# Moving two additions from VectorE to GpSimd in a four-layer graph network, with a new pace, the overflow test ahead of the last normalisations, and layer 2's first loads ahead of the general path

## The chip, the cores and the metric

The kernel runs on one core of one Trainium2 chip. The metric is the device time in microseconds; the kernel before took 4518.02 us (median of 3 runs, 4509.77 to 4524.34). TensorE is written PE, VectorE DVE, ScalarE ACT, GpSimd POOL and SyncE SP, as in the profile.

## The reference

Four graph layers run over N = 2708 nodes with C = 128 features and a sparse adjacency matrix `adj` (2708 x 2708, f32, about five non-zero entries per row). Each layer is `x = x + L(relu(layernorm(x)))`.

```
L0: d = adj.sum(1); (adj * d^-1/2 rows and columns) @ (h @ W + b)
L1: q, k, v = (h @ W.T).reshape(128, N, 8)          # 128 heads of width 8
    a = softmax(q k^T / sqrt(128) + 2 adj);  out = (a v) @ Wo.T
L2: agg = adj.T @ h / deg;  y = agg @ Wn.T + bn + h @ Wc.T + bc
    relu(batchnorm(y) over the nodes)
L3: for each pair (i, j): s = sum_f sigmoid(a_j + b_i + b1) * adj_ij;  sum_j s * h_j;  @ weight + bias
```

The rest of this text is about layer 1 and the start of layer 2.

## The kernel before, in words

Rows of nodes are cut into NT = 22 tiles of 128 (the last has 20). Layer 1 does not form the N x N attention of a head. Its logits are small, so exp(q.k) is replaced by a polynomial: each key is expanded into 128 features (`fk`), each query likewise (`fq`), a head's keys and values become one moment matrix, and the queries are evaluated against it. What the adjacency adds, exp(2 adj) - 1 at the few neighbours of a node, is summed apart, from gathered rows. A test at the end of the layer asks whether the logits and the neighbour counts stayed within the polynomial's limits; if not, three hardware loops (`tc.For_i` with a count of 0 or more, read from `flag`) do the layer again in general form. With these inputs the counts are zero.

**The head loop** (L1106 to L1163) is written out by hand under `tc.manual_schedule()`, so each engine gets its instructions in program order. It has D = 128 heads of NCH = 6 rounds ("chunks", at most four row tiles each). GpSimd makes the key features of head d+2 in round 0 (`keys`, L1015, `mul_g`, L1010) and the products `y` of keys and values in rounds 2 and 5 (`with_values`, L1021). TensorE accumulates the moments of head d+1 (`moments`, L1048), transposes query features (`turn`, L1074) and evaluates head d (`evaluate`, L1086). VectorE weights the moments (`mw`, L1058), makes query features (`fq`, L1007) and, per round, multiplies what was evaluated by the query terms (`z`, L1094) and sums it (`o_raw`, L1100). ScalarE copies transposed features out of PSUM (`fT`, L1076). For every four heads GpSimd adds the sum of the values (`sums`, L693) and SP stores the group (`o_g`).

**Side work** is a chain of Python generators, `first` (L956 to L959). Per round `PACE` steps of it are taken, one step being the code up to the next `yield` (L1150 to L1154). It has four parts in this order:

- `search` and `by_node`, by turns: ten row tiles of adjacency are searched for their largest entries on VectorE (`neighbours`, L128), and q, k and v are stored again by node, 32 groups of heads.
- `in_order` sorts the nodes by their number of neighbours.
- `from_neighbours` (L802) handles 121 slots; slot e of a row tile is the e-th neighbour of its nodes. A slot is: `load` of the next slot (indirect gather on GpSimd's queue, L825, three buffers), `logits` (product `c_z`, L840, and sum `c_c`, L844, both VectorE), and `values` of the slot before (a copy on ScalarE into the ninth column, L869; the product `c_v`, L870; and, except for the first slot of a tile, the addition `c_acc + c_v`, L878, on VectorE). `weigh` (L852, L854) is ScalarE's. A finished tile's `c_acc`, which has one buffer, is scattered to `more_n` (L887, GpSimd's queue). `c_z` and `c_v` share one tag with two buffers.

When `first` is used up, each round takes up to three calls of `step` (L975) on `beside`, a list of two kinds of work: `normalise(g)` (L917) for a group of four heads and `project_out` (L496) for a row tile. `normalise` loads the group and the neighbours' part (L921, L922), adds them (L930, VectorE), takes the reciprocal (L932), multiplies (L933) and stores with twelve or thirteen transfers (L399). `project_out` loads a tile (L499), multiplies with Wo (L505) and adds to `x_sb` (L508). A group may only be normalised once the loop is two groups beyond it, at most two pieces of work are under way, and each has to wait `WAIT = 3` rounds after its loads. What is left when the heads are done is taken after the loop (L1164).

**After the loop** come the test (L1183 to L1225: small reductions on VectorE with five transposes or products on TensorE), the reading of `flag` by all engines, the three loops of the general path (L1229, L1241 to L1295, L1295), and layer 2: loads of two weight matrices and four vectors, `norm_relu` (L192), the reciprocal degrees `di`, 22 steps that spread them over a matrix (`dg` on VectorE, `d_ps` on TensorE, `diB` on ScalarE, L1329 to L1332), and the aggregation `adj.T @ h`: 22 row tiles of adjacency (1354 KB each, four buffers, L1339) against `h` (L1341).

Outside `manual_schedule` blocks the scheduler of the framework chooses each engine's order, within the dependences.

Of the kernel before, what the change touches and what calls it, by code (L numbers as in the profile page):

```python
# [9 lines left out]
FP = mybir.dt.float32  # L10
# [6 lines left out]
P = 128  # L17
# [32 lines left out]
def gnn4_kernel(  # L50
# [75 lines left out]
    few = keep.tile([P, 1], FP, name="few")  # L126

# [388 lines left out]
    with ExitStack() as ph:  # L516
# [285 lines left out]
        def from_neighbours():  # L802
# [55 lines left out]
            def values(b):  # L858
# [6 lines left out]
                for e in range(w):  # L865
# [10 lines left out]
                    yield  # L876
                    if s0 + e:
                        nc.vector.tensor_tensor(acc[:sz], acc[:sz], z[:sz], ALU.add)  # L878
                        yield
# [37 lines left out]
        def normalise(g):  # L917
# [12 lines left out]
            nc.vector.tensor_tensor(ro, ro, co, ALU.add)  # L930
# [67 lines left out]
        PACE = 1.30  # L998
# [107 lines left out]
        with tc.manual_schedule():  # L1106
# [19 lines left out]
            for d in range(D):  # L1126
# [35 lines left out]
                if (d + 2) % GRP == 0 and (d + 2) // GRP + 1 < NG:  # L1162
                    soon.append(prepare((d + 2) // GRP + 1, got))  # L1163
            while beside or under_way:  # L1164
                if not step(n, NG):
                    n += 1


    with ExitStack() as ph:
        gp = ph.enter_context(tc.tile_pool(name="l1g", bufs=1))  # L1170
        gw = ph.enter_context(tc.tile_pool(name="l1g_w", bufs=2))
        g_l = ph.enter_context(tc.tile_pool(name="l1g_l", bufs=1, space=PSUM))
        g_t = ph.enter_context(tc.tile_pool(name="l1g_t", bufs=1, space=PSUM))
        g_o = ph.enter_context(tc.tile_pool(name="l1g_o", bufs=1, space=PSUM))
        q_f = dram.tile([N, P, HEAD], FP, name="q_f")
        k_f = dram.tile([N, P, HEAD], FP, name="k_f")
        v_f = dram.tile([N, P, VW], FP, name="v_f")
        o_f = dram.tile([N, P, HEAD], FP, name="o_f")

        nc.vector.memset(top, 0.0)  # L1183
        p2 = gp.tile([C, 2], FP, name="p2")
        for e in range(2):
            pt = g_t.tile([P, BK], FP, name="g_tr", tag="tr")
            nc.tensor.transpose(pt[:C, :P], most2[:, e], ident)
            nc.vector.tensor_reduce(p2[:, e : e + 1], pt[:C, :P], axis=AX.X, op=ALU.max)
        nc.vector.tensor_tensor(top[:, 0:1], p2[:, 0:1], p2[:, 1:2], ALU.mult)
        nc.vector.tensor_tensor(top[:, 1:2], p2[:, 0:1], p2[:, 1:2], ALU.max)  # L1190
        nc.vector.tensor_reduce(top[:, 2:3], nval, axis=AX.XY, op=ALU.max)
        nc.vector.tensor_reduce(top[:, 3:4], nval, axis=AX.XY, op=ALU.min)
        low = gp.tile([P, 1], FP, name="low")
        nc.vector.tensor_reduce(low, least, axis=AX.X, op=ALU.min)
        nc.vector.tensor_tensor(top[:, 3:4], top[:, 3:4], low, ALU.min)
        nc.vector.tensor_scalar_mul(top[:, 3:4], top[:, 3:4], -1.0)
        nc.vector.tensor_reduce(low, below, axis=AX.X, op=ALU.max)
        nc.vector.tensor_tensor(top[:, 3:4], top[:, 3:4], low, ALU.max)
        nc.vector.tensor_tensor(top[:, 3:4], top[:, 3:4], full, ALU.max)
        pt = g_t.tile([P, BK], FP, name="g_tr", tag="tr")  # L1200
        nc.tensor.transpose(pt[:4, :P], top, ident)
        t4 = gp.tile([4, 1], FP, name="top4")
        nc.vector.tensor_reduce(t4, pt[:4, :P], axis=AX.X, op=ALU.max)
        pt = g_t.tile([P, BK], FP, name="g_tr", tag="tr")
        nc.tensor.transpose(pt[:1, :4], t4, ident[:4, :4])
        bnd = gp.tile([1, 6], FP, name="bound")
        nc.vector.tensor_copy(bnd[:, :4], pt[:1, :4])
        nc.vector.tensor_scalar(
            bnd[:, 4:5], bnd[:, 0:1], MAX_LOGIT**2, None, ALU.is_le
        )  # L1210
# [391 lines left out]
```

## Time and profile before

| what | value |
|---|---|
| median of 3 runs | 4518.02 us (4509.77 to 4524.34) |
| the profiled execution | 4486.52 us, span 4484.7 us |
| mean granted TensorE clock | 0.837 |
| busy, share of the span: PE / DVE / ACT / POOL | 72% / 82% / 25% / 57% |
| first and last start of `mw` (heads 0 and 127) | 465.7 and 3907.1 us |
| first `c_z`, last `c_acc` | 1383.0 and 3524.0 us |
| first and last addition of a normalisation (L930) | 3543.5 and 3999.9 us |
| last addition to `x_sb` of layer 1 (L508) | 4018.1 us |

The spans come from one profiled execution, which was 0.7% faster than the median of the three timed runs; sums made from the profile are sums against 4486.52. The busy share is an average over stages with different limits, so the stages are looked at one by one. In a row of a group, "busy" is the sum over all instructions of the group, "mean ns" one of them, and what follows the bar is how long the engine was idle just before these instructions and what ended that. [...] Line numbers are those of the kernel before; in the kernel after, the lines up to the head loop stand one further down.

### The profile page before, as it was taken

How to read it: one execution, taken by the hardware profiler on the slowest of the kernel's cores; microseconds unless marked ns; L12 is line 12 of the kernel's file. 1: busy time of each engine (PE TensorE's matmuls, PEld its weight loads, DVE VectorE, ACT ScalarE, POOL GpSimd, SP SyncE). 2: the span in 40 equal slices, each digit the busy share in tenths (PEclk: the TensorE clock that was granted, in tenths of full speed). 3: DMA queues.
4: the chain of work that ended last, by engine and by line, in shares of the span. 5: the costliest groups of instructions: out<-in, count | busy, mean ns of one | idle time of the engine just before them, and what ended most of it. 6: DMA issues, size and time to landing. Idle time of an engine off the chain costs nothing. (4 is left out here: it accounts for less than half of the span.)

```text
span 4484.7 us, 49573 instructions
## 1 busy us (share of the span) xinstructions
PE 3225.3 (72%) x17298; PEld 2876.7 (64%) x17298; DVE 3669.4 (82%) x4983; ACT 1100.2 (25%) x2497; POOL 2544.8 (57%) x2253
## 2 busy tenths in 40 slices
PE   7985778889966677677777676667676687839634
PEld 5952777788856666667666676667666677824323
DVE  5988889998868999999999998999899888831323
ACT  4255233334412222222222222222122111101201
POOL 0001766678858666677676676767576555300076
PEclk9987888999988888888888888888888788959555
DMA  4647334357702222222222222222222344447132
GB/s 186 227 154 294 86 101 110 87 126 171 164 9 84 79 75 76 89 81 83 87 76 88 77 92 78 85 86 94 86 88 88 76 97 95 107 108 262 51 100 79
DMA packets 402005, 480.24 MB, mean 107 GB/s; under 512 B 290672, under 2 KB 322098, under 8 KB 376916
## 3 DMA queue, kind: packets, MB, share of 16 engines
q1 hardware_dynamic: 370140, 308.03, 23.8%
q0 software_dynamic: 31600, 168.86, 11.2%
q8 instruction: 144, 2.36, 0.2%
q14 instruction: 121, 0.99, 0.1%
HBM read 363.13 MB, written 113.67 MB: 106 GB/s over the span
## 5 line engine op out<-in xcount | busy, mean ns | idle before, releaser
L1086 PE MATMUL g_ps<-mw,fT 128*128 128x189 f32 x5632 | 1213.3, 362 | 734.6 <-DVE mw L1058 501.9
L1086 PEld LDWEIGHTS g_ps<-mw,fT 128*128 128x128 f32 x5632 | 1032.8, 213 | 812.8 <-issue 642.2
L1010 POOL TENSOR_TENSOR y<-bk,raw 128x2079 f32<-128x2079 f32 x256 | 982.9, 3840 | 685.7 <-PE m_ps L1048 658.4
L1048 PE MATMUL m_ps<-y,fk 128*128 128x189 f32 (+1 forms) x5632 | 1108.1, 342 | 29.0 <-POOL y L1010 29.0
L1048 PEld LDWEIGHTS m_ps<-y,fk 128*128 128x128 f32 (+1 forms) x5632 | 969.2, 204 | 58.1 <-POOL y L1010 29.5
L1076 ACT COPY fT<-f_ps 128x512 f32<-128x512 f32 (+1 forms) x768 | 422.9, 551 | 1955.2 <-PE f_ps L1074 1954.3
L1094 DVE TENSOR_TENSOR z<-g_ps,bq 128x756 f32<-128x756 f32 (+1 forms) x768 | 669.1, 871 | 177.7 <-PE g_ps L1086 173.9
L1100 DVE TENSOR_REDUCE o_raw<-z 128x36 f32<-128x756 f32 (+1 forms) x768 | 672.5, 876 | 26.3
L1010 POOL TENSOR_TENSOR fk<-bk,raw 128x528 f32<-128x528 f32 (+1 forms) x512 | 526.5, 1058 | 0.0
L1074 PE MATMUL f_ps<-ident,fq 128*128 128x128 f32 x2816 | 490.8, 299 | 46.2 <-DVE fq L1007 44.6
L1074 PEld LDWEIGHTS f_ps<-ident,fq 128*128 128x128 f32 x2816 | 399.2, 157 | 83.9 <-issue 45.8
L1010 POOL TENSOR_TENSOR fk<-raw,bk 128x352 f32<-128x352 f32 (+1 forms) x512 | 337.3, 688 | 0.0
L840 DVE TENSOR_TENSOR c_z<-c_kv,c_q 128x1024 f32<-128x1024 f32 (+1 forms) x121 | 308.1, 2546 | 5.3 <-DMA c_kv<-kv_n,srt 5.3
L1007 DVE TENSOR_TENSOR fq<-bq,q_ps 128x528 f32<-128x528 f32 (+1 forms) x512 | 288.1, 605 | 0.0
L825 POOL DMA_INDIRECT c_kv<-kv_n,srt x121 | 139.1, 1150 | 244.3 <-DVE c_v L870 142.4
L1010 POOL TENSOR_TENSOR bk<-raw 128x88 f32<-128x88 f32 (+1 forms) x512 | 238.3, 496 | 34.6 <-DMA raw<-qkv_c 34.1
L878 DVE TENSOR_TENSOR c_acc<-c_acc,c_v 128x1152 f32<-128x1152 f32 (+1 forms) x99 | 248.2, 2507 | 2.5
L465 POOL MEMSET qkv<- 128x512 f32 x6 | 6.3, 1076 | 373.7 <-PE l_o L350 254.3
L870 DVE TENSOR_TENSOR c_v<-c_kv,c_c 128x1024 f32<-128x1024 f32 (+1 forms) x99 | 205.9, 2080 | 0.0
L1420 POOL DMA_INDIRECT g<-gate_d,srt x121 | 122.0, 1008 | 107.9 <-issue 105.1
L505 PE MATMUL l_o<-woT,o_cr 128*128 128x128 f32 (+1 forms) x352 | 94.8, 425 | 107.6 <-DMA o_cr<-o_c 68.6
L1007 DVE TENSOR_TENSOR fq<-q_ps,bq 128x352 f32<-128x352 f32 (+1 forms) x512 | 171.7, 378 | 0.0
(284 smaller groups left out, 3490.2 us busy)
## 6 DMA issues: line engine op xcount, KB each, us to landing
a_nat<-in_adj_dram SPq DMA_DIRECT2D x32, 1354.0 KB
qkv_c<-qkv SPq DMA_DIRECT2D x5, 6400.0 KB
a<-in_adj_dram SPq DMA_DIRECT2D x21, 1354.0 KB
kv_n<-n_kv SPq DMA_DIRECT2D x32, 672.0 KB
an<-in_adj_dram SPq DMA_DIRECT2D x15, 1354.0 KB
o_g<-o_raw SPq DMA_DIRECT2D x32, 396.0 KB
r_raw<-o_g SPq DMA_DIRECT2D x32, 396.0 KB
r_more<-more_n SPq DMA_DIRECT2D x32, 396.0 KB
```

Source lines behind the costliest of these rows:

```text
L825: nc.gpsimd.indirect_dma_start(out=kvs[b][:sz, e].rearrange("p c e k -> p (c e k)"), out_offset=None, in_=kv_n.rearrange("n c k -> n (c k) ...
L840: nc.vector.tensor_tensor(z[:sz], kvs[b][:sz, e, :, 0], qs[t][:sz], ALU.mult)
L870: nc.vector.tensor_tensor(z[:sz, :, :HEAD], kv[:sz, e, :, 1], c[:sz, e, :, None].to_broadcast([sz, C, HEAD]), ALU.mult,)
L878: nc.vector.tensor_tensor(acc[:sz], acc[:sz], z[:sz], ALU.add)
L1007: nc.vector.tensor_tensor(o, x, y, ALU.mult)
L1010: nc.gpsimd.tensor_tensor(o, x, y, ALU.mult)
L1048: nc.tensor.matmul(pms[d][:, : B_ALL * VW], fks[d][:sz, t], ys[d, h][:sz, m].rearrange("p k b -> p (k b)"), start=t == 0, stop=t == NT - 1,)
L1074: nc.tensor.transpose(pt[:, m], fqs[d][:, t0 + m], ident)
L1076: nc.scalar.copy(fts[d, c][:, :n], pt[:, :n])
L1086: nc.tensor.matmul(pg[:, m, : B_ALL * VW], ft[:, m], mws[d].rearrange("p k b -> p (k b)"), start=True, stop=True,)
L1094: nc.vector.tensor_tensor(z[:, :n], pg[:, :n, : B_ALL * VW].rearrange("p t (k b) -> p t k b", k=VW), bqs[d % 2][:, t0 : t0 + n, None, :B_A ...
L1100: nc.vector.reduce_sum(ros[g][:, t0 : t0 + n, i], z[:, :n], axis=AX.X,)
```

## The change

- The neighbours' addition `c_acc + c_v` and the normalisations' addition `r_raw + r_more` are issued to GpSimd instead of VectorE. In `values` the two yields now stand ahead of the addition, so that it is issued one step later than before, and a tile's first slot has a second step as well.
- `PACE` is 1.53 instead of 1.30.
- The test is issued right after the head loop, ahead of the normalisations and projections that are left, with its tiles in pools of the head loop; `flag` is kept for the whole kernel.
- Layer 2's pools are opened before the general path, whose pools lie inside them. Layer 2's weights, vectors, reciprocal degrees with their 22 spreading steps, and the first four adjacency tiles are issued ahead of the general path; `norm_relu` and the aggregation stay behind it.

```diff
@@ values @@
                     yield
+                    yield
                     if s0 + e:
-                        nc.vector.tensor_tensor(acc[:sz], acc[:sz], z[:sz], ALU.add)
-                        yield
+                        nc.gpsimd.tensor_tensor(acc[:sz], acc[:sz], z[:sz], ALU.add)
@@ normalise @@
-            nc.vector.tensor_tensor(ro, ro, co, ALU.add)
+            nc.gpsimd.tensor_tensor(ro, ro, co, ALU.add)
             yield
@@ the head loop @@
-        PACE = 1.30
+        PACE = 1.53
...
                     soon.append(prepare((d + 2) // GRP + 1, got))
+
+            nc.vector.memset(top, 0.0)
+            p2 = sm.tile([C, 2], FP, name="p2")
...
+            nc.vector.tensor_scalar(flag[:, 0:1], bnd[:, 4:5], -1.0, 1.0, ALU.mult, ALU.add)
+            nc.vector.tensor_scalar(
+                flag[:, 1:2], bnd[:, 4:5], -float(C), float(C), ALU.mult, ALU.add
+            )
             while beside or under_way:
                 if not step(n, NG):
                     n += 1
@@ the general path and layer 2 @@
     with ExitStack() as ph:
         lp = ph.enter_context(tc.tile_pool(name="l2", bufs=1))
         wk_pool = ph.enter_context(tc.tile_pool(name="l2w", bufs=2))
         ap = ph.enter_context(tc.tile_pool(name="l2_adj", bufs=4))
+        natural = []
+
+        def rows_of_adj2(t):
+            r0, sz = rows[t]
+            a = ap.tile([P, N], FP, name="a2")
+            nc.sync.dma_start(a[:sz], adj[r0 : r0 + sz])
+            natural.append(a)
+
+        with tc.tile_pool(name="l2_ps0", bufs=2, space=PSUM) as ps:
+            wnT = transposed(lp, wk_pool, ps, wn2, "wnT")
+            wcT = transposed(lp, wk_pool, ps, wc2, "wcT")
+            bias = column_of(lp, bn2, "bn2_sb")
...
+            nc.vector.reciprocal(di, di)
+            diB = lp.tile([P, N], FP, name="diB")
+            for t, (r0, sz) in enumerate(rows):
+                dg = lp.tile([P, P], FP, name="dg", tag="dg", bufs=2)
+                nc.vector.tensor_scalar_mul(dg[:sz, :sz], ident[:sz, :sz], di[:sz, t : t + 1])
+                pd = ps.tile([P, BK], FP, name="d_ps", tag="tr")
+                nc.tensor.matmul(pd[:, :sz], ones[:sz], dg[:sz, :sz], start=True, stop=True)
+                nc.scalar.copy(diB[:, r0 : r0 + sz], pd[:, :sz])
+        for t in range(min(4, NT)):
+            rows_of_adj2(t)
+
+        with ExitStack() as gh:
+            gp = gh.enter_context(tc.tile_pool(name="l1g", bufs=1))
...
+            once = nc.values_load(flag[:, 0:1], min_val=0, max_val=1)
+            heads = nc.values_load(flag[:, 1:2], min_val=0, max_val=C)
+
+            with tc.For_i(0, once):
...
         ps = ph.enter_context(tc.tile_pool(name="l2_ps", bufs=2, space=PSUM))
-        wnT = transposed(lp, wk_pool, ps, wn2, "wnT")
...
         h, hT = norm_relu(lp, ps, "2")
...
             for t, (r0, sz) in enumerate(rows):
-                a = ap.tile([P, N], FP, name="a2")
-                nc.sync.dma_start(a[:sz], adj[r0 : r0 + sz])
+                if t >= len(natural):
+                    rows_of_adj2(t)
+                a = natural[t]
```

## The prediction

> **What bounds the kernel now.** I cut the span into its stages and read the busy time of each engine in each stage (time, busy us and count for PE, weight loads, DVE, ACT and POOL, then the granted PE clock, DMA share and GB/s):
>
> ```profile
> 450.00:950.00 500.00, 395.00 (x2280) 372.00 (x2281) 454.59 (x627) 151.77 (x293) 329.94 (x301) 0.89 0.36 94
> 950.00:1225.00 275.00, 259.51 (x1648) 245.24 (x1646) 234.41 (x397) 116.50 (x226) 228.91 (x213) 1.00 0.74 168
> 1225.00:1383.00 158.00, 101.10 (x562) 94.21 (x561) 98.96 (x159) 25.88 (x58) 110.30 (x124) 0.83 0.15 39
> 1383.00:3524.00 2141.00, 1510.99 (x8221) 1416.40 (x8222) 2038.03 (x2432) 481.67 (x1216) 1474.16 (x1216) 0.84 0.24 82
> 3524.00:3932.00 408.00, 323.52 (x1748) 306.04 (x1746) 331.72 (x492) 65.77 (x151) 206.05 (x174) 0.88 0.45 102
> 3932.00:4018.00 86.00, 27.48 (x112) 25.24 (x112) 26.18 (x48) 0.00 (x0) 2.40 (x1) 0.54 0.52 123
> 4018.00:4048.00 30.00, 4.67 (x17) 2.97 (x17) 14.13 (x91) 4.38 (x13) 0.13 (x1) 0.53 0.37 136
> 4048.00:4157.00 109.00, 108.75 (x322) 54.11 (x320) 11.12 (x38) 8.23 (x34) 0.00 (x0) 0.99 0.65 235
> ```
>
> The rows are: adjacency searches; rearranging by node; ordering the nodes; the neighbours; normalisations inside the head loop; those left after it; the test and the start of layer 2; layer 2's aggregation. The neighbours take 2141 us and VectorE is busy 2038 of them (95%), GpSimd 69%, TensorE 71%. That stage is VectorE's. In the aggregation TensorE never rests. The 86 and 30 us have no busy engine: they are chains of transfers and waits.
>
> The groups say what it does there (count, busy us, mean ns, idle us before):
>
> ```profile
> L840 DVE TENSOR_TENSOR c_z<-c_kv,c_q 128x1024 f32<-128x1024 f32 (+1 forms) x121 | 308.1, 2546 | 5.3 <-DMA c_kv<-kv_n,srt 5.3
> ...
> L878 DVE TENSOR_TENSOR c_acc<-c_acc,c_v 128x1152 f32<-128x1152 f32 (+1 forms) x99 | 248.2, 2507 | 2.5
> ...
> L870 DVE TENSOR_TENSOR c_v<-c_kv,c_c 128x1024 f32<-128x1024 f32 (+1 forms) x99 | 205.9, 2080 | 0.0
> ...
> L693 POOL TENSOR_TENSOR o_raw<-o_raw,v_sum 128x792 f32<-128x792 f32 x32 | 72.4, 2263 | 158.8 <-DVE o_raw L1100 158.8
> ```
>
> The addition's own row, asked by its tile (count: min/median/max ns, first and last start):
>
> ```profile
> L878 DVE TENSOR_TENSOR c_acc<-c_acc,c_v x99: 1337/1754/8283, 1415.0 to 3524.0; 128x1152 f32<-128x1152 f32 x98, 20x1152 f32<-20x1152 f32 x1
> ```
>
> The addition's minimum is 1.34 us and its mean 2.51: about half of it is waiting. The longest took 8.3 us. The other two-input products, L840 and L870, wait likewise.
>
> GpSimd's waits (total us, times, longest):
>
> ```profile
> POOL c_kv L825 <- DVE c_v L870: 142.4, 50, 9.3
> ...
> POOL c_kv L825 <- DVE c_acc L870: 69.3, 15, 8.7
> ```
>
> GpSimd often reaches a gather before VectorE has freed its buffer, so it runs ahead of VectorE. That is its slack.
>
> The end of layer 1 in order of time:
>
> ```profile
> 4018.14 0.28 DVE L508 TENSOR_TENSOR x_sb<-x_sb,l_o 20x128 f32<-20x128 f32 x1 [0.28 <-PE l_o L505]
> ...
> 4022.94 0.13 DVE L1223 TENSOR_SCALAR flag<-bound 1x1 int32<-1x1 f32 x1
> 4032.78 0.13 POOL L197 MEMSET mv<- 128x44 f32 x1 [98.38 <-PEq L1295]
> ```
>
> Test 4.8 us, then 9.8 us for reading the flags and passing three loops.
>
> [...] L840, L870 and L878 have minima of 1.2 to 1.3 us and means of 2.1 to 2.5, while L1094, with one input in PSUM, never exceeds 0.97. [...] L693 (1.85 us at best for 792) scales to 2.7. [...]
>
> **Pace (1.30 to 1.53).** There are 128 heads of 6 rounds, 768 rounds. Counting the yields, the side work has 272 steps of searches and rearranging (searches end near step 160), 30 of ordering and 587 of neighbours: 889. At 1.30 that is 684 rounds; 114 heads, and 14 are left for normalising, which is what the trace shows. The second yield in the values is now taken by the 22 first slots too: 609 and 911 in all, at 1.53 in 595 rounds. The stages become 17.4, 12.2, 3.3, 66.3 and 28.8 heads, where they were 20.5, 14.4, 3.9, 75.3 and 14.
>
> **Neighbours' additions.** In that stage VectorE's records sum to 2153 us: 1214 for 75.3 heads (16.1 each) and 939 for 121 neighbour slots. Busy time is 0.947 of the sum, since records overlap. Without the additions (243.9) a slot costs (308.1+146.7+205.9+34.1)/121 = 5.74. New sum: 66.3x16.1 + 121x5.74 = 1762, busy 1669. [...] GpSimd's share of the stage goes from 69% to: (1474 less 195 of DMA work)/75.3 = 17.0 a head, x66.3 = 1127, +195, + 99 additions at 2.7 to 3.2 (the upper end is L693's mean, scaled) = 1589 to 1639, near 88%. VectorE's 242 remaining two-input operations wait about 1.1 us each now. I scale with GpSimd's share and allow for the new 2.7 us holder: 0.35 us more each, 85 us. 1754 busy, at 95.2% is 1843 us, 27.8 a head. Bounds: no more waiting, 1753 us; GpSimd's own queue, below. The added waits I cost at nothing, and say what covers each: a gather (3.6/5.8/10.5 us from issue to landing) is issued five steps, 3.3 rounds or 15 us, ahead of its use; ScalarE's next copy into the c_v buffer (L869) comes three steps, 9 us, behind the addition that must free it, and behind that copy stand the fT copies for TensorE; the store of a finished row tile (L887) is on GpSimd's queue, and the next first product already waits 49 us in all for it to land. Two us of lag at each of 22 stores would be 44 us, inside the bounds. The stage changes by -298, of which heads moved out of the stage come back in the next.
>
> **Other stages of the loop.** Searches: VectorE does 3.1 heads fewer, 454.6 - 47 = 407, at the old 91% 448: -52. Rearranging: 12.2 heads at 19.1 = 233; the same transfers in less time raise the DMA share from 0.74 to 0.87, for which I add 10 (ends 0 and 25): -32. Ordering: -11. Normalising: ahead of it lie 36 projections and normalisations that are due at once, and the old stage did about 40 in 14 heads at 29.1 us, so 13.5 heads are dense. There each addition leaves VectorE (1.59 us in that stage) but the reciprocal queued behind it now waits until GpSimd has finished a key or y product and the addition (1.9): about 3 us, net 1.5, near two a head. Behind that reciprocal stand the next z products, and TensorE waits for them. 13.5x31.1 = 420. The other 15.3 heads have almost no side work; the rearranging stage ran 19.1 a head with the array at full clock; 20.5 gives 314. Together 734, +326 (ends +270 and +410). Loop: -52-32-11-298+326 = -67.
>
> **After the loop.** The last groups that may be normalised inside stay 30 and 31, plus four projections; before, 7 and 7 were left, 86 us. Now: flags and first loop 9 (in which the first load lands), addition, reciprocal, product 3.5, twelve stores 4.8, next load 5.6, the same again 8.3, loads and two projections 11: about 43. -43. The test lies in there beside transfers; without that cover it costs its 4.8. But the order of instructions shows that di and 22 dg/d_ps/diB steps, which ran beside the aggregation at about 0.65 us each, now stand between the last projection and the second loop: +14. Test gone from the path -4.8, one loop of three past -3, the 3 us VectorE waited for wnT -3: the 30 become about 33. Of the four early adjacency loads two are queued on SP before the second loop, two after the third; the stage is TensorE's, which loses the 22 d_ps products: -6. End: -46.
>
> **Sum.** 4486.5 (the profiled execution; span 4484.7) - 67 - 46 = 4373. The median shown is 0.7% above that execution; 4373x4518.0/4486.5 = 4405.
>
> **Rivals.** (a) The port waits do not grow, since the addition that blocked is itself gone: stage 1753, -90: 4315. For it: L878 alone waited 1.17 us each, 116 us, and collisions come from y, not from small products. Against: GpSimd near 90%. (b) Slower: GpSimd's queue becomes the bound. An addition waits for the c_v product two steps before, and behind it in that in-order queue stand gathers, keys and y, for which TensorE waits. Work 1640 us; if 121 gathers and 99 additions each wait 1.9 us as gathers do now (212/113), 418 us more: 2058, +215: 4620. It decides from 1.4 us each (1843+113-1640 = 316 over 220). Against: GpSimd then lags and its waits shrink. (c) The reciprocal's wait spoils the tail: dense heads at 35, light ones at 24: +105, 4510, no change to be seen. That the early test doesn't move is excluded by the instruction order: the first loop stands before the last additions on all queues.
>
> **Chances.** Forecast (4350 to 4460) 0.48, (a) 0.27, (c) 0.13, (b) 0.12. The range leaves out the low end of (a) and most of (b): 4310 to 4530. Measurement can tell 0.3% (14 us) from no change: faster 0.78, same 0.08, slower 0.14.
>
> **What would show it.** L878's successor on GpSimd near 2.7 to 3.2 us; neighbours' stage ends near 3130 us of the span instead of 3524; c_z and c_v means near 2.9 and 2.4; fewer than 60 us from the last o_raw to the last projection; diB before the aggregation. A neighbours' stage over 1956 us, or light heads over 24, makes it wrong.

## The result, and the profile after

| | before | after |
|---|---|---|
| median of 20 runs each | 4523.2 us | 4499.5 us |
| ratio after/before | | 0.9946, 95% interval 0.9929 to 0.9963 |
| profiled execution, span | 4484.7 us | 4492.1 us |
| neighbours' stage, first c_z to last addition | 1383 to 3524 | 1293 to 3260 |
| last o_raw to last projection (the drain) | 86.6 us | 44.8 us |

The changed kernel is 0.54% faster (24 us). The direction was forecast, the size was not: 4405 us, 2.5% less, had been forecast. The measured time lies inside the range of 4310 to 4530. One of the 20 runs before took 7724 us, which moves that median by 1 us. The profiled execution of the kernel before was a quick one (0.8% under its median of 20), that of the changed kernel is 0.1% under its own; so the two traces together hide the small gain, and only ratios of times say below which kernel is faster. The traces are used for where time is spent.

The busy time by stage of the changed kernel (time, busy us and count for PE, weight loads, DVE, ACT and POOL, then granted clock, DMA share, GB/s). The rows are the neighbours, the rest of the head loop, the end of the normalisations, the start of layer 2 and its aggregation:

```profile
1293.00:3259.00 1966.00, 1352.30 (x7229) 1266.70 (x7230) 1860.67 (x2094) 439.90 (x1117) 1524.53 (x1197) 0.82 0.26 88
3259.00:3968.00 709.00, 603.69 (x3453) 571.97 (x3452) 544.87 (x884) 138.23 (x318) 482.15 (x406) 0.92 0.33 75
3968.00:4012.00 44.00, 16.71 (x67) 14.38 (x68) 12.64 (x45) 0.00 (x0) 5.48 (x3) 0.53 0.40 100
4012.00:4042.00 30.00, 10.65 (x57) 7.79 (x56) 16.03 (x88) 9.59 (x34) 0.13 (x1) 0.77 0.51 190
4042.00:4147.00 105.00, 105.00 (x280) 49.95 (x279) 6.40 (x18) 3.35 (x14) 0.00 (x0) 0.97 0.63 227
```

The neighbours' stage took 1966 us where 1843 was forecast. VectorE is still its bound: 1861 of 1966 us busy, 95% as before, although the 99 additions (248 us) have left it. GpSimd is at 78%, TensorE at 69%. VectorE's idle time, 105 us, is what it was (103), so neither TensorE's granted clock (0.84 before, 0.82 here) nor a transfer explains the miss. The tail (the head loop behind the neighbours) took 709 us (734 forecast), the drain 44.8 (43), the start of layer 2 30 (33), the aggregation 105 (103): these came as reckoned.

Where VectorE's time went is in the groups (count, busy us, mean ns, idle us before and what ended it):

```profile
L841 DVE TENSOR_TENSOR c_z<-c_kv,c_q 128x1024 f32<-128x1024 f32 (+1 forms) x121 | 440.0, 3636 | 9.4 <-DMA c_kv<-kv_n,srt 9.4
...
L871 DVE TENSOR_TENSOR c_v<-c_kv,c_c 128x1024 f32<-128x1024 f32 (+1 forms) x99 | 269.4, 2721 | 4.4 <-POOL c_acc L880 4.4
L880 POOL TENSOR_TENSOR c_acc<-c_acc,c_v 128x1152 f32<-128x1152 f32 (+1 forms) x99 | 261.0, 2637 | 180.9 <-DVE c_v L871 152.7 <-issue 13.8 <-ACT fT L1077 9.3
```

c_z grew from 2546 to 3636 ns and c_v from 2080 to 2721. The work is the same, and so are the minima, but the median of c_z has more than doubled (count: min/median/max ns, first and last start; before, then after):

```profile
L840 DVE TENSOR_TENSOR c_z<-c_kv,c_q x121: 1212/1585/9812, 1383.0 to 3508.3; 128x1024 f32<-128x1024 f32 x119, 20x1024 f32<-20x1024 f32 x2
L841 DVE TENSOR_TENSOR c_z<-c_kv,c_q x121: 1209/3650/14601, 1293.0 to 3242.3; 128x1024 f32<-128x1024 f32 x119, 20x1024 f32<-20x1024 f32 x2
```

With the first products (34.1 to 36.8 us), which a tile's first slot writes straight into c_acc, that is 198 us more on VectorE, against the 248 us of additions that left it. The additions' own row says that GpSimd did them at a steady price, just under the 2.7 to 3.2 us reckoned:

```profile
L880 POOL TENSOR_TENSOR c_acc<-c_acc,c_v x99: 2596/2626/3601, 1325.3 to 3260.1; 128x1152 f32<-128x1152 f32 x98, 20x1152 f32<-20x1152 f32 x1
```

GpSimd's waits in the stage (total us, times, longest) have changed places. It now stands for c_v, for the sake of the addition, and much less for the buffers of the gathers and for TensorE's moments (335.5 us before); its idle time has gone from 667 to 441 us:

```profile
POOL c_acc L880 <- DVE c_v L871: 152.7, 59, 7.0
POOL y L1011 <- PE m_ps L1049: 145.5, 48, 9.2
POOL c_kv L826 <- DVE c_acc L871: 51.0, 13, 6.6
```

One piece of the timeline shows the growth (start, us, engine, line; VectorE and GpSimd of the changed kernel):

```profile
2008.33 2.63 POOL L880 TENSOR_TENSOR c_acc<-c_acc,c_v 128x1152 f32<-128x1152 f32 x1 [1.23 <-DVE c_v L871]
...
2011.10 0.97 POOL L826 DMA_INDIRECT c_kv<-kv_n,srt  x1
...
2012.09 3.78 POOL L1011 TENSOR_TENSOR y<-bk,raw 128x2079 f32<-128x2079 f32 x1
...
2013.23 11.18 DVE L841 TENSOR_TENSOR c_z<-c_kv,c_q 128x1024 f32<-128x1024 f32 x1
2015.82 1.37 POOL L1011 TENSOR_TENSOR bk<-raw 128x176 f32<-128x176 f32 x4
2017.16 2.36 POOL L1011 TENSOR_TENSOR fk<-raw,bk 128x352 f32<-128x352 f32 x4
2019.49 3.83 POOL L1011 TENSOR_TENSOR fk<-bk,raw 128x528 f32<-128x528 f32 x4
...
2024.34 0.34 DVE L1059 TENSOR_TENSOR mw<-m_ps,W 128x189 f32<-128x189 f32 x1
```

The product needs 1.2 us and took 11.2. It began 1.1 us into y, and it ended 1.1 us after the last key product: it was kept out not for the one instruction that it met but for thirteen in a row. The addition itself had ended 2.3 us before it began. All 11.2 us count as busy time of VectorE. Behind it stood mw, and behind mw TensorE, idle for 12.6 us.

The end of layer 1, in order of time: the flags, the last normalisation but one, the last projection. The flags are now computed ahead of the last normalisations:

```profile
3974.50 0.13 DVE L1207 TENSOR_SCALAR flag<-bound 1x1 int32<-1x1 f32 x1
3978.65 1.87 POOL L931 TENSOR_TENSOR r_raw<-r_raw,r_more 128x792 f32<-128x792 f32 x1 [8.89 <-SPq L1266]
...
4012.32 0.28 DVE L509 TENSOR_TENSOR x_sb<-x_sb,l_o 20x128 f32<-20x128 f32 x1 [0.29 <-PE l_o L506]
```

### The profile page after: what moved, and what is told of

Same layout as the page of the kernel before. It is cut to its first block, busy times and chain, and to the rows that moved or that the text cites. A ratio compares the mean times of both kernels' runs of the same rounds, so it can differ in the third digit from the quotient of the medians.

```text
span 4492.1 us, 49603 instructions
## 1 busy us (share of the span) xinstructions
PE 3238.8 (72%) x17298; PEld 2887.0 (64%) x17298; DVE 3592.1 (80%) x4852; ACT 1102.6 (25%) x2497; POOL 2781.9 (62%) x2384
## 5 line engine op out<-in xcount | busy, mean ns | idle before, releaser
L1087 PE MATMUL g_ps<-mw,fT 128*128 128x189 f32 x5632 | 1228.1, 366 | 741.1 <-DVE mw L1059 378.2
L1087 PEld LDWEIGHTS g_ps<-mw,fT 128*128 128x128 f32 x5632 | 1043.4, 215 | 823.8 <-issue 526.6
L1011 POOL TENSOR_TENSOR y<-bk,raw 128x2079 f32<-128x2079 f32 x256 | 972.9, 3801 | 544.8 <-PE m_ps L1049 523.5
L1011 POOL TENSOR_TENSOR fk<-bk,raw 128x528 f32<-128x528 f32 (+1 forms) x512 | 507.8, 1020 | 0.0
L841 DVE TENSOR_TENSOR c_z<-c_kv,c_q 128x1024 f32<-128x1024 f32 (+1 forms) x121 | 440.0, 3636 | 9.4 <-DMA c_kv<-kv_n,srt 9.4
L880 POOL TENSOR_TENSOR c_acc<-c_acc,c_v 128x1152 f32<-128x1152 f32 (+1 forms) x99 | 261.0, 2637 | 180.9 <-DVE c_v L871 152.7
L1011 POOL TENSOR_TENSOR fk<-raw,bk 128x352 f32<-128x352 f32 (+1 forms) x512 | 316.4, 646 | 0.0
L871 DVE TENSOR_TENSOR c_v<-c_kv,c_c 128x1024 f32<-128x1024 f32 (+1 forms) x99 | 269.4, 2721 | 4.4 <-POOL c_acc L880 4.4
L1011 POOL TENSOR_TENSOR bk<-raw 128x88 f32<-128x88 f32 (+1 forms) x512 | 223.5, 467 | 33.6 <-DMA raw<-qkv_c 33.3
L845 DVE TENSOR_REDUCE c_c<-c_z 128x128 f32<-128x1024 f32 (+1 forms) x121 | 146.8, 1213 | 3.5 <-DVE c_z L841 0.5
```

Source lines behind the costliest of these rows:

```text
L841: nc.vector.tensor_tensor(z[:sz], kvs[b][:sz, e, :, 0], qs[t][:sz], ALU.mult)
L845: nc.vector.reduce_sum(cs[b][:sz, e], z[:sz], axis=AX.X)
L871: nc.vector.tensor_tensor(z[:sz, :, :HEAD], kv[:sz, e, :, 1], c[:sz, e, :, None].to_broadcast([sz, C, HEAD]), ALU.mult,)
L880: nc.gpsimd.tensor_tensor(acc[:sz], acc[:sz], z[:sz], ALU.add)
L1011: nc.gpsimd.tensor_tensor(o, x, y, ALU.mult)
L1087: nc.tensor.matmul(pg[:, m, : B_ALL * VW], ft[:, m], mws[d].rearrange("p k b -> p (k b)"), start=True, stop=True,)
```

## The experiments

Three theories. **A, the port:** the additions on GpSimd hold up VectorE's two-input products. "Port" is only my word for what the two engines would then exclude each other from; no trace shows such a thing, the waits alone are measured. In the trace before, the 88 products that began while GpSimd ran nothing waited 0.7 us together, the 144 that began under one of its reading instructions 230 us. **B, the queue:** the additions stand in GpSimd's queue, wait there for c_v, and make keys, y and gathers late. **C, pace and order:** the pace of 1.53 or the place of the steps ate the gain, not the additions.

All ratios are against the kernel before, run on the same chip beside each kernel; between chips its median moved from 4497 to 4523 us, so ratios are compared here and not times. A point is 0.01 of a ratio; line numbers are each run's own. "Product waits" below (the "port waits" of the recorded texts) are the sum of the groups c_z, c_v and first products less 242 times 1.21 us; "idle" is the stage less VectorE's busy time, the stage being counted to the issue of the last finished sum. How far one trace can be trusted is seen where two kernels have the same neighbours' stage: 2146 and 2170 us with product waits of 255 and 261 (the kernel before, and the end of layer 1 alone), 1970 and 1964 us with 453 and 440 (the changed kernel, and the one with the normalisation's addition back on VectorE).

### The addition left out

```diff
-                    if s0 + e:
-                        nc.gpsimd.tensor_tensor(acc[:sz], acc[:sz], z[:sz], ALU.add)
```

> Leaves out the 99 neighbours' additions (the sum then holds the first slot's product alone); every step of the order is kept. Theory A, the port [...]: c_z falls from 3.64 us to 2.5 or below and c_v from 2.72 to 2.1 or below, some 198 us of VectorE time in the neighbours' stage, which becomes 1966 - 170 to 200 = about 1780 us; the whole is 0.95 to 0.96 of before (4300 to 4345). Theory B, the queue (additions delay keys, y and gathers behind them): also faster, but c_z and c_v keep most of their length (over 3.2 and 2.4), and what goes is idle time of PE and VectorE. Theory C (PACE and the order around it, not the additions, ate the gain): within 1% of the changed kernel, 0.985 to 1.0 of before.

Measured: 4352.0 us, ratio 0.9613 (0.9578 to 0.9648). The stage is 1812 us.

```profile
L841 DVE TENSOR_TENSOR c_z<-c_kv,c_q 128x1024 f32<-128x1024 f32 (+1 forms) x121 | 317.1, 2621 | 8.0 <-DMA c_kv<-kv_n,srt 8.0
L871 DVE TENSOR_TENSOR c_v<-c_kv,c_c 128x1024 f32<-128x1024 f32 (+1 forms) x99 | 236.6, 2390 | 0.0
```

So an addition that cost nothing would have given 1812 us, and the forecast of 1843 had left only 31 us for 99 additions. They cost 158. Product waits are 304 us here and 453 in the changed kernel: 149 of the 158. C falls as the main cause. And even with no additions anywhere, the waits stay above those of a kernel that has them on VectorE (255 us before; 233 us at the pace of 1.53, in a later run). VectorE's own additions wait too (116 us of their 248 before), so it seems that the next product meets some of those collisions when they leave. c_z stayed above the 2.5 us and c_v above the 2.1 that theory A had expected.

### Memsets in place of the addition

```diff
-                        nc.gpsimd.tensor_tensor(acc[:sz], acc[:sz], z[:sz], ALU.add)
+                        for part in (z[:sz], z[:sz], z[:sz, : C // 2]):
+                            nc.gpsimd.memset(part, 0.0)
```

> Leaves out the neighbours' additions and puts in their place three memsets of the dead c_v tile (1152, 1152 and 576 elements, about 2.7 us together, as long as the addition's 2.64, and waiting for c_v as it did): GpSimd's queue is as full, but the new work reads nothing from SBUF. Theory A, the port by way of operations that read: like the kernel without the addition to within 1%, c_z 2.6 or below. Theory B, the queue: like the changed kernel to within 1% (0.985 to 1.0 of before). If memsets hold the port as well as additions do, c_z stays at 3.4 or over with GpSimd's waits unchanged; that would leave A right as to the port and wrong as to the reading.

Measured: 4476.4 us, ratio 0.9883 (0.9848 to 0.9919): within 1% of the changed kernel, 2.8% from the kernel without the addition. The stage is 1955 us, product waits 409. c_z, at 3.07 us, lies between the marks set for it (2.6 and 3.4).

```profile
L841 DVE TENSOR_TENSOR c_z<-c_kv,c_q 128x1024 f32<-128x1024 f32 (+1 forms) x121 | 370.9, 3065 | 10.0 <-DMA c_kv<-kv_n,srt 10.0
L871 DVE TENSOR_TENSOR c_v<-c_kv,c_c 128x1024 f32<-128x1024 f32 (+1 forms) x99 | 298.9, 3020 | 4.4 <-POOL c_v L881 4.4
```

The memset itself held nothing up; its timeline:

```profile
2740.50 2.83 POOL L881 MEMSET c_v<- 128x1152 f32 x3
2741.08 1.23 DVE L841 TENSOR_TENSOR c_z<-c_kv,c_q 128x1024 f32<-128x1024 f32 x1
```

The 16 c_z that began under memsets, which read nothing, waited 0.2 us together; the 35 that began under y, which reads two tiles, waited about 100 us in the same trace. Yet the products wait almost as long as in the changed kernel: of the 149 us that the addition adds to the product waits, 105 come with memsets too. So theory A was half wrong: VectorE's products do wait for GpSimd, but what an addition does and a memset doesn't makes at most the other 44 us of it. I then sorted every c_z of the neighbours' stage by the GpSimd instruction under which it began:

| c_z begun under | no addition: count, mean wait | changed kernel: count, mean wait |
|---|---|---|
| y | 52, 2.11 us | 40, 3.38 us |
| key products (fk) | 31, 1.61 us | 24, 3.02 us |
| a gather's issue | 4, 0.0 us | 14, 3.57 us |
| the addition | none | 15, 1.09 us |

Under the addition itself VectorE lost 16 us. For the rest, each wait of the 242 products can be split at the end of the reading GpSimd instruction under which the product began (where there was none, the whole wait counts as behind it):

| kernel | products begun under one | wait for that one, us | wait behind it, us |
|---|---|---|---|
| before | 144 | 147 | 108 |
| no addition | 167 | 167 | 137 |
| memsets | 143 | 166 | 244 |
| in the change | 159 | 187 | 266 |

So 129 of the 149 us lie behind the instruction that was met: the products did not meet GpSimd oftener, but were kept out over more of its instructions in a row. Waits of over 5 us, longer than any one of these instructions, number 9 without the addition and 24 with it. The growth is in products begun under keys (101 to 156 us behind the one met) and under a gather's issue (4 to 54 us); those begun under y were kept out little longer behind it (21 to 30 us), and their longer mean above comes mostly from beginning earlier in y.

This is B's cause acting through A's waits, as far as the records go: work that fills GpSimd's queue, reading or not, makes VectorE lose to several instructions. Which gaps it closes is seen only in part. With less than 0.4 us between, GpSimd went from a gather to y 38 of 92 times without the addition and 60 of 92 with it, from keys to y 10 and 15 of 24 times, from y to keys 33 times in both. How much is owed to the length of GpSimd's runs and how much to the moment in them at which a product begins is not separated here. Why one such boundary lets VectorE in and another doesn't, the records don't show; that stays open.

### The addition that waits for nothing

```diff
-                        nc.gpsimd.tensor_tensor(acc[:sz], acc[:sz], z[:sz], ALU.add)
+                        nc.gpsimd.tensor_tensor(acc[:sz], acc[:sz], acc[:sz], ALU.subtract)
```

> The addition reads the sum alone (sum minus sum, two SBUF inputs of the same size, so the neighbours' contribution is left out) and so no longer waits for c_v: [...] the queue isn't held for 152.7 us. Theory A: within 0.8% of the changed kernel, c_z 3.4 or over. Theory B: faster than the changed kernel by 50 us or more (0.984 of before or less), because y, keys and gathers come earlier.

Measured: 4458.8 us, ratio 0.9855 (0.9824 to 0.9885), 0.9% from the changed kernel: between the two expectations. c_z fell to 2835 ns, under A's bound, but c_v rose to 3233; product waits are 408 us. The instruction was also shorter, 2.39 us against 2.64. The wait for c_v is thus worth at most the 32 us by which this stage is shorter (1938 us, where the changed kernel has 1970), which is hardly more than two traces of one stage differ, and the shorter instruction is in that. Behind the instruction met, the products wait 242 us, nearly as long as with the addition (266).

### The addition two steps later

Each addition is issued after the next slot's c_z, in `logits`, instead of ahead of it: `added()` issues what `owing` holds.

```diff
...
             yield
+            added()
             nc.vector.reduce_sum(cs[b][:sz, e], z[:sz], axis=AX.X)
...
-                        nc.gpsimd.tensor_tensor(acc[:sz], acc[:sz], z[:sz], ALU.add)
+                        owing.append((acc, z, sz))
```

> The changed kernel with each neighbours' addition issued after the next slot's c_z instead of ahead of it (two steps later), so GpSimd does not stand for c_v. Theory A: the queue is still as full, and keys and y still come in long runs; what goes is the 153 us for which GpSimd stood for c_v and the 16 us for which c_z waited under an addition: 15 to 60 us faster than the changed kernel, 0.981 to 0.991 of before, c_z 2.7 to 3.4 us. Rival (it is the distance between the addition and c_z that costs): c_z at 2.6 or below and 0.975 or less.

Measured: 4510.9 us, ratio 1.0023 (1.0011 to 1.0035): slower than the changed kernel, a miss. GpSimd no longer stood for c_v at all, but c_z was as long as ever (3704 ns), product waits stayed at 433 us, and a new wait came: c_v for the addition that frees its buffer, in VectorE's waits:

```profile
DVE c_v L879 <- POOL c_acc L840: 62.3, 18, 7.7
```

So neither the standing for c_v nor the nearness of addition and c_z is what makes the product waits.

### The addition back on VectorE

```diff
                     yield
-                    yield
                     if s0 + e:
-                        nc.gpsimd.tensor_tensor(acc[:sz], acc[:sz], z[:sz], ALU.add)
+                        nc.vector.tensor_tensor(acc[:sz], acc[:sz], z[:sz], ALU.add)
+                        yield
```

> The changed kernel with only the neighbours' addition back on VectorE (at its old place, five steps for a slot in both); pace 1.53, normalisation's addition on GpSimd and the early test and layer 2 loads stay. Theory A: VectorE takes 99 additions back and loses the lengthened products, so the stage is about 28.4 us per head for 66 heads plus the unchanged base work spread on fewer heads, 2000 to 2080 us against 1966; the whole is 0.3 to 2.5% slower than the changed kernel (0.997 to 1.02 of before). Theory C (moving the additions is worth nothing or less, the gain of the whole came from the other parts): same or faster than the changed kernel, 0.985 to 0.9945.

Measured: 4562.1 us, ratio 1.0092 (1.0054 to 1.0129). Moving the additions is therefore worth 1.5 points at this pace (1.0092 to 0.9946), as A expected, and the rest of the change without it loses 0.9. The stage is as long as in the changed kernel (1965 us; 2000 to 2080 had been expected) but holds 2.4 heads fewer, since the 22 first slots have one step less ((22/1.53)/6); product waits are 233 us.

### Steps kept off the chunks with the long runs

```diff
-                    owed += PACE
+                    owed += (0.0, 2.2, 2.0, 3.0, 2.0, 0.0)[c]
```

> The changed kernel with the same number of steps for a head (9.2) but given by chunk: none in the first and the last of the six, where GpSimd runs y and the next keys back to back, and 2.2, 2, 3, 2 in the four between. In the changed kernel's trace the products begun in the first and last chunk waited 3.10 and 2.62 us each (231 us of 453), those of the others 0.87 to 1.79. Theory A: the waits fall by 60 to 120 us and the stage with them: 0.968 to 0.984 of before. Rival (the runs shift with the steps, or GpSimd's bunched gathers and additions become the bound): 0.99 or more.

Measured: 4574.0 us, ratio 1.0162 (1.0139 to 1.0185): the forecast of the time missed, that of the waits held. Product waits fell from 453 to 342 us. But VectorE's idle time in the stage rose from 106 to 239 us, because it now ran ahead of TensorE in the two chunks without side work: its waits for what TensorE evaluates, all but 0.6 us of them at the products z that come first after those chunks, were in the changed kernel and are here:

```profile
DVE z L1095 <- PE g_ps L1087: 38.7, 40, 1.7
DVE z L1095 <- PE g_ps L1087: 143.8, 122, 2.7
```

The side steps are also what VectorE does while TensorE evaluates a chunk; bunched, they no longer fill that time.

### The pace back at 1.30

```diff
-        PACE = 1.53
+        PACE = 1.30
```

> The changed kernel with the pace put back to 1.30 steps a chunk. Theory A, as the first runs left it (VectorE sets the neighbours' stage, and its two-input products wait behind runs of keys and y that a fuller GpSimd queue makes longer): 17 heads go back from the light tail (20 us each) into the stages, where one more head costs some 16.5 us, and the additions meet fewer runs per us; 20 to 90 us faster than the changed kernel, 0.975 to 0.990 of before. Theory C' (the higher pace is what makes the additions pay): slower than the changed kernel, 0.998 or more of before.

Measured: 4499.1 us, ratio 0.9998 (0.9978 to 1.0018): slower than the changed kernel, as C' had it, and for a reason that I had not reckoned. The head loop ends 91 us earlier, but the 11.2 heads left in the tail are too few for the normalisations, and 156 us of drain follow with every engine mostly idle:

```profile
3541.00:3876.00 335.00, 254.10 (x1369) 239.99 (x1367) 237.54 (x370) 51.48 (x118) 190.40 (x152) 0.86 0.43 96
3876.00:4032.00 156.00, 46.38 (x180) 41.86 (x180) 35.70 (x94) 0.00 (x0) 22.51 (x13) 0.54 0.51 118
```

### The end of layer 1 alone

The kernel before with the early test, layer 2's loads and diB ahead of the general path; both additions on VectorE, pace 1.30. Against the changed kernel:

```diff
                     yield
-                    yield
                     if s0 + e:
-                        nc.gpsimd.tensor_tensor(acc[:sz], acc[:sz], z[:sz], ALU.add)
+                        nc.vector.tensor_tensor(acc[:sz], acc[:sz], z[:sz], ALU.add)
+                        yield
...
-            nc.gpsimd.tensor_tensor(ro, ro, co, ALU.add)
+            nc.vector.tensor_tensor(ro, ro, co, ALU.add)
...
-        PACE = 1.53
+        PACE = 1.30
```

> The kernel before with the last two parts alone (the test ahead of the remaining normalisations, layer 2's loads and diB ahead of the general path); both additions on VectorE and the pace at 1.30. If the end of layer 1 is worth what the two traces show up to the end of the aggregation (from the last o_raw to there 224.8 us before, 178.9 after): 46 us faster than before, 0.988 to 0.992. Then the other three parts together cost the changed kernel about 22 us. Rival: layer 2's later waits take it back (the changed kernel's lead at the aggregation was gone by the end in its profiled run): 0.996 to 1.0.

Measured: 4508.8 us, ratio 1.0018 (1.0002 to 1.0034): no gain, and just outside the rival's 0.996 to 1.0. My expectation had read the shorter end of the changed kernel's trace as the work of these two parts. It is the pace's: here the drain is 90 us, as before (86.6), against 44.8 in the changed kernel; the kernel before with the pace alone at 1.42, below, has 40.9. From the last projection to layer 2's first residual sum the parts save 4 us (155.7 to 151.8).

### The normalisation's addition back on VectorE

```diff
-            nc.gpsimd.tensor_tensor(ro, ro, co, ALU.add)
+            nc.vector.tensor_tensor(ro, ro, co, ALU.add)
```

> The changed kernel with only the normalisation's addition back on VectorE; the neighbours' additions stay on GpSimd. In the changed kernel the reciprocal waited 54 us in all for it (23 times) while VectorE was 77% busy in that tail. If that wait delays the heads behind it (my rival c in small): 10 to 40 us faster than the changed kernel, 0.986 to 0.993 of before. If the 1.6 us that each of 32 additions takes from VectorE weigh as much: within 0.3% of the changed kernel, 0.992 to 0.998.

Measured: 4476.3 us, ratio 0.995 (0.9934 to 0.9967), the same as the changed kernel's 0.9946. Which engine does it makes no difference that these intervals, 0.2 points either way, can tell.

### The addition as an adding transfer

A transfer that GpSimd issues does the addition here, into c_acc as it lands. That left GpSimd only the issue, 0.94 us each.

```diff
-                        nc.gpsimd.tensor_tensor(acc[:sz], acc[:sz], z[:sz], ALU.add)
+                        nc.gpsimd.dma_start(
+                            out=acc[:sz].rearrange("p c k -> p (c k)"),
+                            in_=z[:sz].rearrange("p c k -> p (c k)"),
+                            accum_op=ALU.add,
+                        )
```

> The changed kernel with the neighbours' addition done by a transfer that GpSimd issues and that adds c_v to the sum as it lands, so nothing is left out; GpSimd is held for the issue alone, about 1 us by the gathers' 0.97, instead of 2.64[...]. Theory A: keys and y come sooner and in shorter runs; c_z falls from 3.64 to between 2.6 (no addition) and 3.2, c_v below 2.9, and the neighbours' stage to 1820 to 1890 us: 0.965 to 0.982 of before. Rival: landing takes so long that the c_v buffer and the finished sums come late, which gives the gain back: 0.99 or more, with c_v waiting for the transfer.

Measured: 4409.3 us, ratio 0.9804 (0.9782 to 0.9826), with nothing left out.

```profile
L841 DVE TENSOR_TENSOR c_z<-c_kv,c_q 128x1024 f32<-128x1024 f32 (+1 forms) x121 | 327.8, 2709 | 11.7 <-DMA c_kv<-kv_n,srt 11.7
L871 DVE TENSOR_TENSOR c_v<-c_kv,c_c 128x1024 f32<-128x1024 f32 (+1 forms) x99 | 238.0, 2404 | 24.8 <-DMA c_acc<-c_v 24.8
L880 POOL DMA_DIRECT2D c_acc<-c_v x99 | 93.0, 940 | 187.4 <-issue 58.9 <-DVE c_v L871 44.1 <-ACT fT L1081 20.3
```

GpSimd is held 0.94 us for an addition, and the product waits are back at 310 us, where they were without any addition (304); behind the instruction met they are 148 us (137 without). From a gather to y GpSimd still went with less than 0.4 us between 55 of 92 times, so that count alone doesn't tell how long VectorE waits. The stage, 1890 us, is at the upper end of what was expected, 78 above the kernel without additions: VectorE idles 165 us of it instead of 97, in part for landings (24.8 us here, and first products for their stores 59.3 instead of 35.8).

The kernels at a pace of 1.53, side by side:

| addition | GpSimd, us each | stage, us | VectorE busy | idle | product waits |
|---|---|---|---|---|---|
| none | 0 | 1812 | 1715 | 97 | 304 |
| adding transfer | 0.94 | 1890 | 1726 | 165 | 310 |
| sum minus sum | 2.39 | 1938 | 1821 | 117 | 408 |
| memsets | 2.69 | 1955 | 1822 | 133 | 409 |
| in the change | 2.64 | 1970 | 1864 | 106 | 453 |

### The pace with the transfers, and with neither

The pace alone was changed, to 1.42 and 1.64 with the adding transfers, then to 1.42 in the changed kernel and (there from 1.30) in the kernel before.

```diff
-        PACE = 1.53
+        PACE = 1.42
```

> The kernel with the adding transfers at a pace of 1.42 instead of 1.53. 46 rounds (7.7 heads) go back from the tail into the stages. From the run of the changed kernel at 1.30, which ended its head loop 92 us sooner but then needed 156 us instead of 45 to the last projection, the tail needs about its 29 heads for the normalisations: the loop ends some 40 us sooner and the drain grows by 25 to 55 us; within 0.4% of the same kernel at 1.53, 0.977 to 0.985 of before. Rival (pace matters by itself): 0.970 or less, or 0.99 or more.

> The kernel with the adding transfers at a pace of 1.64: 40 rounds (6.7 heads) go from the stages to the tail, where no normalisation is left to fill them; at 1.53 the drain is 45 us already and cannot fall much. A head costs about 17 us in the stages and 18 to 20 in the tail, and port waits rise as the base work comes closer together: 10 to 50 us slower than at 1.53, 0.982 to 0.992 of before. Rival (stages gain more than the tail loses): 0.978 or less.

Measured: at 1.42 4353.5 us, ratio 0.9652 (0.9612 to 0.9693), the best of the kernels that leave nothing out; at 1.64 4482.5, ratio 0.995 (0.9933 to 0.9966). Both expectations missed. At 1.64 the loss was larger than reckoned (1.5 points, where 0.2 to 1.2 had been expected). At 1.42 the rival's mark, 0.970 or less, came: the drain did not grow (44.7 us, as at 1.53 and 1.64). The tail has 21.1 heads at 1.42 (128 less 911/1.42/6), and those still hold all the normalisations; the 28.8 at 1.53 were more than they need. The two traces show only 30 us between 1.53 and 1.42, less than half of what the ratios do (1.5 points, 68 us); the profiled run at 1.42 was the slowest of its four, that at 1.53 nearly the fastest of its six.

> The changed kernel at a pace of 1.42, the additions on GpSimd's arithmetic as in the change. With the adding transfers, going from 1.53 to 1.42 took 56 us off, since the tail of heads shrank from 28.8 to 21.1 and still held all normalisations (drain 45 us in both). If the change's pace of 1.53 is what ate part of its gain: 30 to 60 us faster than the changed kernel, 0.981 to 0.988 of before. If the gain at 1.42 belongs to the transfers alone (at 1.30 the changed kernel was 0.5% slower than at 1.53): 0.993 to 1.0.

> The kernel before with the pace alone at 1.42. Its stage is VectorE's with the additions on it, so heads pushed out of the stages (9.7 of them, at 16 us) cost 24 us each in the tail, and the drain falls from 87 to some 45 us: 15 to 55 us slower, 1.003 to 1.012. If the right length of the tail is worth as much by itself as with the changed kernel: 0.985 to 0.995 of before, and then the additions' move is worth next to nothing at any pace.

Measured: the changed kernel at 1.42 4446.2 us, ratio 0.9893 (0.9865 to 0.992), about half a point under its 0.9946 at 1.53, a little less than the 30 us at which the expectation began. The kernel before at 1.42: 4493.0, ratio 0.9998 (0.9981 to 1.0014); a longer loop took back what the drain gave (40.9 us), so this one missed on both sides. At the pace of 1.42 the rest of the change is worth 1.05 points.

In the traces of the changed kernel, going from 1.53 to 1.42 lengthens the stages ahead of the neighbours by 38 us for 2.5 heads and the neighbours' stage by 71 us for 5.2 heads (14 to 15 us a head), and shortens the tail from 705 to 562 us for 7.7 heads (19 us a head). Here a head was cheaper beside side work than in a tail that has none left.

## Why the prediction was right in sign and wrong in size

**Counts, pace, stages ahead of the neighbours: right.** The neighbours begin at 1293 us (1288 by the forecast's sums); the tail (709 for 734) and the pieces behind it up to the aggregation's end came within 25 us of the forecast together.

**The failed step** is the term "0.35 us more each, 85 us" for the products' waits. It scaled the mean wait with GpSimd's share of the stage, as if only the number of collisions could grow and each ended with the instruction that is met. Measured: (453 - 255)/242 = 0.82 us more each, 198 us, of which 158 lie behind the instruction met (108 to 266). The excess, 113 us, is nearly the whole of the stage's miss (1966 against 1843). It is also close to that of the forecast on the profiled executions (4494 against 4373), since the other errors cancel: 5 us ahead of the neighbours, -24 behind them, and 17 behind the aggregation, in code that the change doesn't touch (the part behind the first residual sum of layer 2 took 311 to 337 us in all these traces).

The trace of before already held the sign. Products of 1.2 us lasted up to 9.8 us (the c_z row shown with the profile after), and y, the longest reading instruction, takes 3.8: they were kept out over several instructions in a row (that of 9.8 us began 1.2 us before y's end and ended 1.1 us after the last of twelve key products). That length grew with the work given to GpSimd, and GpSimd's share rose less than reckoned (to 78%, not 88%), as its work was less (1525 us for 1589 to 1639) and the stage longer.

**Rival (a)**, no longer waits at all, 1753 us for the stage: not even the kernel without additions gets there (1812): its product waits are 304 us, and 233 at the same pace with the additions on VectorE. Nor did the collisions come from y alone: 81 of the 255 us before began under keys (fk). **Rival (b)**, GpSimd's queue as the bound: its mark, a stage over 1956 us, was passed, yet its mechanism isn't there as it was put: GpSimd is 78% busy, and taking its wait for c_v away gains little or nothing. It was right in that what fills the queue is the cause; it looked for the cost in late gathers, keys and y, and it lay in VectorE's products. **Rival (c)**, the reciprocal's wait: the total came near its number, 4510, by another way; the run with that addition back on VectorE shows no cost, and the tail was shorter than forecast.

**The addition's price** was nearly right (2.64 us for 2.7 to 3.2; the upper end, L693's mean of 2.26 us scaled from 792 to 1152 elements, comes out at 3.3). **The covers** held in part: c_v waited for its buffer 4.4 us in all, but ScalarE waited 35 us for additions that free that buffer and 182 us for landed sums, where it had 131 before. VectorE's idle time shows no cost of that.

**The end of layer 1:** the drain's 43 us came, by the pace and not by the early test, as the sum had it; the rest of the end gave 4 to 5 us. What the sum did not ask is whether 1.53 was a good pace. It put 28.8 heads into a tail that needs some 21, and that cost the changed kernel about half a point more.

## What to carry to other kernels

Where VectorE's two-input products wait for GpSimd's reading instructions, as here, reckon a collision by how long GpSimd may run such instructions without a gap (here up to 11.2 us for y and twelve key products), not by one instruction and not in proportion to its busy share. It is an upper end, since VectorE got in at some of the boundaries. A maximum well over the partner's longest instruction, in the trace before (here 9.8 us against 3.8), tells that this holds. Work moved to GpSimd can cost VectorE even if it holds no product up itself: the stage grew by 1.6 us for each 2.64 us addition (158/99), and still by 1.4 for memsets of 2.69 (143/99), under which 16 c_z waited 0.2 us; where only the issue had to go there, as for an adding transfer, the cost halved (78 us of stage). After such a move set the pace again by looking at the tail: just enough main work to cover what can only run last.

## What the runs showed of the hardware that was not expected

- A VectorE product of 1.2 us was kept out over y and twelve key instructions without a gap (11.2 us; 14.6 where an addition of o_raw stood between them), though in other places the same product got in between y and the keys. The sign is in the keys: the four small bk products took 1.37 us in the case above and 2.21 to 2.48 in the 34 where VectorE was let in ahead of them.
- GpSimd memsets held no two-input product up (16 of them, 0.2 us), but cost the stage 143 us, 105 of them in longer waits for other instructions.
- A transfer of 576 KB that adds into SBUF as it lands held GpSimd 0.94 us; one issued at 2105.8 us let ScalarE go on at 2114.4, 8.6 us later. The stage with 99 of them had a DMA share of 0.43, where the changed kernel has 0.26, without a visible cost to VectorE's products (310 us of product waits, 304 without any addition).
